# Attention products as four 32-token strips, with the queries turned together with the attention weights

## The chip, the cores and the metric

The kernel runs on one core of a Trainium2 chip, all in float32. The metric is the device time of one execution in microseconds (us); the time before is the median of 12 runs.

## The reference, cut to what matters

Cross-attention and a layer of mixed experts over 4 x 1024 tokens of width 256. The queries come from the normalised tokens, keys and values from a context of 77 rows per batch; 16 heads of 64. Then every token takes two of nine experts (256 to 704 and back).

```python
ln = layernorm(layernorm(x), ln2_w, ln2_b)      # 4 x 1024 x 256: queries
q  = (ln @ Wq) * (1 + scale) + shift            # 16 heads of 64
k, v = split(layernorm(ctx, ln1_w, ln1_b) @ Wkv)
attn = softmax(q @ k.T / 8)                     # 1024 x 77 for each head and batch
x = x + (attn @ v) @ Wout
y = layernorm(x)
x = x + sum over top 2 of 9 experts: w_e * (silu(y @ Wg[e]) * (y @ Wu[e])) @ Wd[e]
```

## The kernel before

**Folded weights.** Before the loop the kernel folds Wq and the keys into one matrix `g` per batch (256 x 1232, plus nine columns for the router), and the values and Wout into `u` (1280 x 265: ten blocks of 128 keys, KC = 10, and 265 = 256 outputs and nine router columns). So for a block of 128 tokens attention is two sets of products: scores = z times `g`, and values = weights times `u`.

**The loop.** There are 32 token blocks (eight groups of four). The instructions stand in the order in which the code calls them; each engine works through its own in that order, and the transfers named here are all issued by SyncE (SP) into one queue. Iteration i does, on TensorE in this order:

- `scores(i, 0)` (L285), six heads of scores, 462 columns;
- `query_turn(i + 1)` (L272), which turns the next block's normalised queries z from tokens by channels into channels by tokens, with two transposing products into `pz`; ScalarE copies them to `zT` (L274), which is the stationary operand of the scores;
- `scores(i, 1)`, `scores(i, 2)` (462 and 317 columns);
- `values(i - 3)` (L361), ten products of 265 columns whose stationary operand is `aT`, the turned attention weights of block i - 3 (LAG = 3).

Iterations 1 to 4 hold left-over preparation too (`extra`): context values and the products for `u` on 64x64 parts of the array. Every fourth iteration has the two small rank products of the router (`ranks`, L1017 and L1020).

Around them: VectorE takes the maxima of the scores (L289); ScalarE the exponentials (L300); VectorE multiplies with the reciprocal sums into the one tile `an` (L322, L327), and `weights_turn(i - 1)` (L341) turns `an` in blocks of 32x32 into `anT`. The turn writes each word ten words from the one before, since the block of keys is the innermost index:

```python
turned = pools["qpool"].tile([P, NQ, Q, KC], F32, tag="anT", name=f"anT{i}", bufs=1)
nc.vector.transpose(
    turned.rearrange("p q t k -> p q k t"), an_of[0].rearrange("p (k q t) -> p q k t", q=NQ, t=Q)
)
nc.sync.dma_start(out=a_d[i % 2], in_=turned.rearrange("p q t k -> p (q t k)"))
```

A turn of 32x32 blocks is not a turn of 128x128, so SyncE stores `anT` to `a_d` in device memory (L344, 640 KB) and `weights_back(i - 1)`, at the end of iteration i, loads it again with the blocks in their places as `aT` (L352, four loads of 160 KB). `aT` has two buffers. Ahead of `weights_back` in SyncE's queue stand, in some iterations, the loads of x (L220), the stores of the sum x (L927) and of the normalised y (L967; these wait for ScalarE), in iteration 1 the 1060 KB of `u_d` (L828), and near the end of the loop the first experts' weights (L1344 to L1354).

`query(i + 2)` (L263) is ScalarE's normalisation of the block after next, into one of two tiles `zs`.

**The experts.** The expert stage (`hidden_pair` L1421, `hidden_thin` L1449, `hidden_one` L1486, `down` L1516) follows the loop and is not changed, apart from the two rank products that fall into it. In `hidden_one` and `down` a block that two or four experts share is worked on in strips of 64 or 32 columns of the array. The strip is chosen by the partitions of the output.

Of the kernel before, what the change touches and what calls it, by code (L numbers as in the profile page):

```python
# [8 lines left out]
F32 = mybir.dt.float32  # L9
I32 = mybir.dt.int32  # L10
U32 = mybir.dt.uint32
AF = mybir.ActivationFunctionType
# [3 lines left out]
P = 128  # L16
# [5 lines left out]
def kernel(  # L22
# [30 lines left out]
    NS = TB // P  # L53
    NG = TOK // TB
    GPB = N // TB
# [3 lines left out]
    JA = 64  # L59
    JR = J - JA  # L60
    NR = 2
    HR = H // NR
    KC = NP + NR
    W = 16
    N2 = NP // 2
    NA = KC * P
    DE = D + E
    HB = TB // J
    banks = [(h, min(HB, H - h)) for h in range(0, H, HB)]
# [46 lines left out]
    ones = const.tile([P, P], F32, name="ones")  # L116
# [76 lines left out]
    pools = {}  # L193


    zs, an_of, lines = [], [], []

    def open_attention():
        for name, bufs in (("qpool", 2), ("rpool", 2)):
            pools[name] = attention.enter_context(tc.tile_pool(name=name, bufs=bufs, side="right"))  # L200
        q = pools["qpool"]
        zs.extend(q.tile([P, D], F32, name=f"z{i}", bufs=1) for i in range(2))
        an_of.append(q.tile([P, NA], F32, name="an", bufs=1))
        for z in zs:
            nc.gpsimd.memset(z[:, D - 1 : D], 1.0)
        for i in range(3):
            lines.append(
                [q.tile([P, NS, WORDS], F32, name=f"line{i}_{k}", bufs=1) for k in range(2)]
            )
            for t in lines[-1]:  # L210
                nc.gpsimd.memset(t.bitcast(I32), NOWHERE)
        for an in an_of:
            nc.gpsimd.memset(an[:, H * JA :], 0.0)

    xg = {}
    pools["xpool"] = attention.enter_context(tc.tile_pool(name="xpool", bufs=4, side="right"))
# [40 lines left out]
    zTs, exs, sms, lgs, aTs, nmx, fstats, pscs = {}, {}, {}, {}, {}, {}, {}, {}  # L257

    def query(i):

        g, s = divmod(i, NS)
        o, r, _ = zscale[g]
        nc.scalar.activation(  # L263
            zs[i % 2][:, : D - 1], xg[g][:, s, : D - 1], AF.Identity,
            bias=o[:, s : s + 1], scale=r[:, s : s + 1],
        )

    def query_turn(i):
# [4 lines left out]
        zT = zTs[i] = pools["qpool"].tile([P, C, P], F32, tag="zT", name=f"zT{i}")  # L273
        nc.scalar.copy(zT.rearrange("p c t -> p (c t)"), pz[:, : C * P])  # L274

    def scores(i, k):

        zT = zTs[i]
        h, n = banks[k]
        if k == 0:  # L280
            nmx[i] = stat.tile([P, H], F32, tag="mx", name=f"mx{i}")
        psc = pscs[k] = ps_sc.tile([P, TB], F32, tag=f"sc{k}", name=f"psc{i}_{k}")
        w = n * J + (E if h + n == H else 0)
        for c in range(C):
            nc.tensor.matmul(  # L285
                psc[:, :w], zT[:, c, :], g_sb[i // NS // GPB][:, c, h * J : h * J + w],
                start=(c == 0), stop=(c == C - 1),
            )
        nc.vector.tensor_reduce(  # L289
            nmx[i][:, h : h + n], psc[:, : n * J].rearrange("p (h j) -> p h j", h=n), AX.X,  # L290
            ALU.max, negate=True,
        )
# [23 lines left out]
    def attention_weights(i):  # L316

        ex, sm = exs.pop(i), sms.pop(i)
        rs = stat.tile([P, H], F32, tag="rs", name=f"rs{i}")
        nc.vector.reciprocal(rs, sm)  # L320
# [6 lines left out]
        nc.vector.tensor_tensor(  # L327
            an[:, H * JA :].rearrange("p (m w n) -> p n m w", w=W, n=N2)[:, :, :, :JR],
            ex[:, :, JA:J].rearrange("p (n m) j -> p n m j", n=N2),
            rs.rearrange("p (n m) -> p n m", n=N2).unsqueeze(3).to_broadcast([P, N2, four, JR]),  # L330
            ALU.mult,
        )

    Q = 32
    NQ = P // Q

    def weights_turn(i):


        turned = pools["qpool"].tile([P, NQ, Q, KC], F32, tag="anT", name=f"anT{i}", bufs=1)  # L340
        nc.vector.transpose(  # L341
            turned.rearrange("p q t k -> p q k t"), an_of[0].rearrange("p (k q t) -> p q k t", q=NQ, t=Q)
        )
        nc.sync.dma_start(out=a_d[i % 2], in_=turned.rearrange("p q t k -> p (q t k)"))  # L344

    def weights_back(i):

        aT = aTs[i] = pools["qpool"].tile([P, NQ, Q * KC], F32, tag="aT", name=f"aT{i}")
        there = a_d[i % 2]
        by_key = there.rearrange("(a i) (q m) -> q i a m", i=Q, q=NQ)  # L350
        for q in range(NQ):
            nc.sync.dma_start(out=aT[q * Q : (q + 1) * Q], in_=by_key[q])  # L352

    pos = {}

    def values(i):
        b = i // NS // GPB
        aT = aTs.pop(i).rearrange("p a (t k) -> p (a t) k", k=KC)
        po = pos[i] = mm_tile(f"po{i}")
        for n in range(KC):  # L360
            nc.tensor.matmul(  # L361
                po[:, :DE], aT[:, :, n], u_sb[b][:, n, :], start=(n == 0), stop=(n == KC - 1)
            )

    def attended(i):
# [15 lines left out]
    with ExitStack() as kvs:  # L381
# [60 lines left out]
        cT = vside.tile([P, C, B * J], F32, name="cT")  # L442
# [121 lines left out]
        for n in range(NP):  # L564
            pk = bank_tile(f"pk{n}")
            for c in range(C):
                nc.tensor.matmul(
                    pk[:, : B * J], wk_sb[:, c, n * P : (n + 1) * P], cT[:, c, :],
                    start=(c == 0), stop=(c == C - 1),
# [5 lines left out]
            while n and pks:  # L575
                m, pk = pks.pop(0)
# [9 lines left out]
            k = n - TURN  # L586
# [50 lines left out]
        def router_weights(pm):  # L637
# [69 lines left out]
        for n in range(NP):  # L707
# [7 lines left out]
            for c in range(C):  # L715
                for t in range(2):
# [4 lines left out]
                        start=True, stop=True,  # L721
                    )
                    h = place_of(n, t)
# [65 lines left out]
        def context_values(k, new=mm_tile):  # L789
            n = k // 2 + k % 2 * N2  # L790
            pv = new(f"pv{n}")
            for c in range(C):
                nc.tensor.matmul(
                    pv[:, : B * J], wv_sb[:, c, n * P : (n + 1) * P], cT[:, c, :],
                    start=(c == 0), stop=(c == C - 1),
                )
# [82 lines left out]
    def rest_of_keys(*ns, last=False):  # L879
# [134 lines left out]
    def ranks(g):  # L1014
        pp = routed[g]["pp"] = mm_tile(f"pp{g}")
        sel, cums = routed[g]["sel"], routed[g]["cums"]
        nc.tensor.matmul(  # L1017
            pp[:, : NS * E], before, sel.rearrange("p s e -> p (s e)"), start=True, stop=False
        )
        nc.tensor.matmul(  # L1020
            pp[:, : NS * E], ones, cums.rearrange("p s e -> p (s e)"), start=False, stop=True
        )

    def places(g):

# [591 lines left out]
        ranks(g)  # L1617
        yield from places(g)

    N_SUB = NG * NS  # L1620
    LAG = 3
    chosen, early = None, None
    for i in range(N_SUB + 1):
        g, s = divmod(i, NS)
# [29 lines left out]
        if now_on:  # L1654
            if i:
                scores(i, 2)
                exponentials(i, 2)
                queries_logits(i)
            if i < N_SUB - 2:
                query(i + 2)  # L1660
            if i:
                extra(i, 2)
            if i == END:
                vsides.close()
        else:
            turn(0)
# [134 lines left out]
```

## Time and profile before

| what | value |
|---|---|
| median of 12 runs | 853.38 us (852.65 to 854.88) |
| the profiled execution: its time, its span | 853.94 us, 852.2 us |
| TensorE granted clock, mean | 0.998 |
| attention loop, scores of iteration 0 to values of block 31 | 36 to 357 us |
| VectorE's turn L341 | 32 of 2.49 us |
| ScalarE's z L263, copy L274 | 32 of 0.61 us, 32 of 0.40 us |
| transfers on SyncE's queue | 158.57 MB, 59.0% of 16 engines' span |

A row of the groups reads: line, engine, operation, output<-inputs, the part of the array (rows*columns, for TensorE), the shape, how many; then busy time and the mean of one in ns; then idle time of the engine in front of them and what ended it. PE is TensorE's products, PEld its weight loads, DVE VectorE, ACT ScalarE, POOL GpSimd, SP SyncE (SPq its DMA queue). A float32 product is two passes in these rows (a transposing product is one). Products are pipelined: the busy mean of one is longer than the step from one start to the next. In a timeline the first number is the start and the second the length, both in us.

### The profile page before, as it was taken

The page shows a single profiled execution, that of the slowest core. Times are in us where ns is not written, and L with a number is a line of the kernel's source. Part 1 is how long each engine was busy: PE and PEld are TensorE (multiplying, and loading weights), DVE is VectorE, ACT ScalarE, POOL GpSimd, SP SyncE. Part 2 cuts the span into 40 slices and gives each one's busy share as a digit, 9 for nine tenths or more (in the row PEclk, how much of TensorE's full clock was granted, in tenths as well). Part 3 has the DMA queues.
Part 4 walks back from the last instruction along what each step waited for, and adds up shares of the span by engine and source line. Part 5 has one row for each costly group of instructions (what it writes and reads, how often), then busy time and mean ns, then how long its engine had stood idle before and what let it go on. Part 6 is the DMA issues. An engine that isn't in the chain of part 4 may idle for free. (4 is left out here: it accounts for less than half of the span.)

```text
span 852.2 us, 14468 instructions
## 1 busy us (share of the span) xinstructions
PE 841.0 (99%) x4148; PEld 674.9 (79%) x4148; DVE 596.4 (70%) x1887; ACT 380.1 (45%) x1570; POOL 311.1 (36%) x344
## 2 busy tenths in 40 slices
PE   8999999999999999999999999999999999999996
PEld 6755877877877878988888879788778878877895
DVE  5777779999989989454854575485578466667550
ACT  4878687978879686252221222222222222222221
POOL 3100000404414140477573454544444453453522
PEclk9999999999999999999999999999999999999999
DMA  8026657566566597896885799789679988788521
GB/s 293 4 108 180 173 180 204 165 218 188 171 195 181 153 264 226 290 306 142 215 240 144 191 339 354 198 238 333 184 225 349 288 224 282 215 246 248 121 25 19
DMA packets 129424, 177.25 MB, mean 208 GB/s; under 512 B 26167, under 2 KB 95295, under 8 KB 129216
## 3 DMA queue, kind: packets, MB, share of 16 engines
q1 hardware_dynamic: 111930, 158.57, 59.0%
q0 software_dynamic: 17344, 17.75, 11.9%
q8 instruction: 33, 0.54, 0.3%
q14 instruction: 47, 0.39, 0.2%
q10 hardware_dynamic: 70, 0.00, 0.0%
HBM read 136.89 MB, written 40.81 MB: 208 GB/s over the span
## 5 line engine op out<-in xcount | busy, mean ns | idle before, releaser
L1421 PE MATMUL pg<-xT,wgu 128*128 128x256 f32 x1100 | 242.7, 379 | 0.1
L1421 PEld LDWEIGHTS pg<-xT,wgu 128*128 128x128 f32 x1100 | 208.5, 190 | 28.7 <-ACT xT L1410 0.7
L1537 POOL DMA_INDIRECT out_dram<-co,ids x73 | 116.0, 1589 | 203.9 <-ACT co L1519 131.1
L300 ACT ACTIVATE ex<-psc,mx 128x77 f32<-128x77 f32 x512 | 159.1, 337 | 64.4 <-DVE mx L289 61.6
L1516 PE MATMUL po<-wd,hid 128*128 128x256 f32 (+2 forms) x768 | 173.2, 380 | 0.0
L1516 PEld LDWEIGHTS po<-wd,hid 128*128 128x128 f32 (+2 forms) x768 | 138.7, 183 | 28.6 <-issue 6.2
L361 PE MATMUL po<-u,aT 128*128 128x265 f32 x640 | 152.2, 393 | 0.8 <-DMA aT<-a_d 0.8
L361 PEld LDWEIGHTS po<-u,aT 128*128 128x128 f32 x640 | 149.6, 311 | 4.1 <-issue 1.7
L1394 DVE STREAM_TRANSPOSE xT<-yin 32x128 f32<-32x128 f32 (+1 forms) x528 | 144.7, 274 | 9.0
L1049 POOL DMA_INDIRECT list_d<-line,r_pli x64 | 66.7, 1042 | 229.8 <-DVE r_pli L1036 120.4
L285 PE MATMUL psc<-g,zT 128*128 128x462 f32 (+1 forms) x384 | 146.7, 513 | 0.0
L1428 DVE TENSOR_TENSOR hid<-pg,sl 128x256 f32<-128x256 f32 x130 | 55.0, 423 | 117.2 <-ACT sl L1427 115.7
L1427 ACT ACTIVATE sl<-pg 128x256 f32<-128x256 f32 x130 | 49.7, 383 | 176.5 <-PE pg L1421 169.5
L300 ACT ACTIVATION_READ_ACCUMULATOR ex<-psc,mx 128x1 f32 x512 | 111.2, 218 | 0.0
L285 PEld LDWEIGHTS psc<-g,zT 128*128 128x128 f32 x384 | 69.7, 190 | 42.9 <-issue 34.3
L1519 ACT ACTIVATE co<-po,ids 128x256 f32<-128x256 f32 x66 | 31.1, 473 | 123.9 <-PE po L1516 121.0
L341 DVE STREAM_TRANSPOSE anT<-an 128x1280 f32<-128x1280 f32 x32 | 79.7, 2492 | 1.9 <-DMA a_d<-anT 1.9
L1361 POOL DMA_INDIRECT yin<-y_d,ids x66 | 69.3, 1051 | 31.6 <-issue 15.6
L289 DVE TENSOR_REDUCE mx<-psc 128x6 f32<-128x462 f32 (+1 forms) x96 | 53.6, 558 | 18.5 <-PE psc L285 18.5
L1506 DVE STREAM_TRANSPOSE hid<-hs 32x160 f32<-32x160 f32 (+1 forms) x112 | 39.5, 353 | 1.7
L322 DVE TENSOR_TENSOR an<-ex,rs 128x1024 f32<-128x1024 f32 x32 | 39.3, 1229 | 1.1
L1449 PEld LDWEIGHTS pt<-xT,wgu 128*128 128x128 f32 x308 | 35.1, 192 | 2.1 <-issue 2.0
(370 smaller groups left out, 766.8 us busy)
## 6 DMA issues: line engine op xcount, KB each, us to landing
wgu<-in_L_ffn_Wg_dram SPq DMA_DIRECT2D x33, 704.0 KB
wd<-in_L_ffn_Wd_dram SPq DMA_DIRECT2D x33, 640.0 KB
a_d<-anT SPq DMA_DIRECT2D x32, 640.0 KB
aT<-a_d SPq DMA_DIRECT2D x128, 160.0 KB
wgu<-in_L_ffn_Wu_dram SPq DMA_DIRECT2D x33, 512.0 KB
w_up<-in_L_ffn_Wg_dram SPq DMA_DIRECT2D x12, 704.0 KB
d_up<-in_L_ffn_Wd_dram SPq DMA_DIRECT2D x12, 640.0 KB
w_up<-in_L_ffn_Wu_dram SPq DMA_DIRECT2D x12, 512.0 KB
```

Of the source, the lines that this page charges most:

```text
L285: nc.tensor.matmul(psc[:, :w], zT[:, c, :], g_sb[i // NS // GPB][:, c, h * J : h * J + w], start=(c == 0), stop=(c == C - 1),)
L289: nc.vector.tensor_reduce(nmx[i][:, h : h + n], psc[:, : n * J].rearrange("p (h j) -> p h j", h=n), AX.X, ALU.max, negate=True,)
L300: nc.scalar.activation(exs[i][:, h + q, :], pscs[k][:, q * J : (q + 1) * J], AF.Exp, bias=nmx[i][:, h + q : h + q + 1], accum_out=sms[i][: ...
L341: nc.vector.transpose(turned.rearrange("p q t k -> p q k t"), an_of[0].rearrange("p (k q t) -> p q k t", q=NQ, t=Q))
L361: nc.tensor.matmul(po[:, :DE], aT[:, :, n], u_sb[b][:, n, :], start=(n == 0), stop=(n == KC - 1))
L1049: i = nc.gpsimd.indirect_dma_start(out=list_d[:, :], out_offset=bass.IndirectOffsetOnAxis(ap=place_i[:, s : s + 1], axis=0), in_=entry.bit ...
L1361: return nc.gpsimd.indirect_dma_start(out=dst, out_offset=None, in_=src, in_offset=bass.IndirectOffsetOnAxis(ap=offsets, axis=0), **kw,)
L1394: yield nc.vector.transpose(xT[q : q + Q].rearrange("p c (h t) -> p h c t", t=P)[:, :nh, :, a : a + Q], of(yins, j)[a : a + Q].rearrange(" ...
L1421: nc.tensor.matmul(pg[:, g, :], w[:, c, at : at + P], xT[:, c, :], start=(c == 0), stop=(c == C - 1),)
L1428: made = nc.vector.tensor_tensor(hid[:, f, :], pg[:, 1, :], sl, ALU.mult)
L1516: nc.tensor.matmul(po[rows, :D], hid[:, f, at], d[:, f, :], start=(f == 0), stop=(f == NF))
L1537: i = nc.gpsimd.indirect_dma_start(out=out_r, out_offset=bass.IndirectOffsetOnAxis(ap=ids[j][:, h, word : word + 1], axis=0), in_=cos[j][: ...
```

## The change

- Scores, values, ranks and most of the context-value products are issued as four products of 32 stationary columns each, one for each strip of 32 tokens (32 rows of the output), all with the same moving operand (`strips`).
- From block 3 on, the normalised queries are not turned by TensorE. ScalarE writes z of block i + 3 into 256 more columns of `an` (KT = KC + C = 12 blocks of 128); VectorE's turn, the store and the loads carry it along, and `scores(i + 3)` read it from `aT` of block i. `query_turn` stays for blocks 0 to 2.
- The turn writes runs of 32 words: the innermost index of `anT` and `aT` is the token in its strip, and no longer the block of keys.

```diff
-    a_d = [dram.tile([P, NA], F32, name=f"a_d{i}") for i in range(2)]
+    a_d = [dram.tile([P, KT * P], F32, name=f"a_d{i}") for i in range(2)]
...
+    def strips(out, left, right, **kw):
+
+        for a in range(0, P, Q):
+            nc.tensor.matmul(out[a : a + Q], left(a), right, **kw)
...
+        z = zs[i % 2] if i < LAG else an_of[0][:, NA:]
...
+    def turned_query(i, c):
+
+        if i < LAG:
+            return lambda a: zTs[i][:, c, a : a + Q]
+        return lambda a: aTs[i - LAG][:, a // Q, KC + c, :]
...
-            nc.tensor.matmul(
-                psc[:, :w], zT[:, c, :], g_sb[i // NS // GPB][:, c, h * J : h * J + w],
+            strips(
+                psc[:, :w], turned_query(i, c), g_sb[i // NS // GPB][:, c, h * J : h * J + w],
...
-        turned = pools["qpool"].tile([P, NQ, Q, KC], F32, tag="anT", name=f"anT{i}", bufs=1)
-        nc.vector.transpose(
-            turned.rearrange("p q t k -> p q k t"), an_of[0].rearrange("p (k q t) -> p q k t", q=NQ, t=Q)
-        )
-        nc.sync.dma_start(out=a_d[i % 2], in_=turned.rearrange("p q t k -> p (q t k)"))
+        turned = pools["qpool"].tile([P, NQ, KT, Q], F32, tag="anT", name=f"anT{i}", bufs=1)
+        nc.vector.transpose(turned, an_of[0].rearrange("p (k q t) -> p q k t", q=NQ, t=Q))
+        nc.sync.dma_start(out=a_d[i % 2], in_=turned.rearrange("p q k t -> p (q k t)"))
...
-        aT = aTs[i] = pools["qpool"].tile([P, NQ, Q * KC], F32, tag="aT", name=f"aT{i}")
+        aT = aTs[i] = pools["qpool"].tile([P, NQ, KT, Q], F32, tag="aT", name=f"aT{i}")
...
         for q in range(NQ):
-            nc.sync.dma_start(out=aT[q * Q : (q + 1) * Q], in_=by_key[q])
+            nc.sync.dma_start(
+                out=aT[q * Q : (q + 1) * Q].rearrange("i a k t -> i a (k t)"), in_=by_key[q]
+            )
...
         for n in range(KC):
-            nc.tensor.matmul(
-                po[:, :DE], aT[:, :, n], u_sb[b][:, n, :], start=(n == 0), stop=(n == KC - 1)
+            strips(
+                po[:, :DE], lambda a: aT[:, a // Q, n, :], u_sb[b][:, n, :],
+                start=(n == 0), stop=(n == KC - 1),
             )
...
-        nc.tensor.matmul(
-            pp[:, : NS * E], before, sel.rearrange("p s e -> p (s e)"), start=True, stop=False
-        )
-        nc.tensor.matmul(
-            pp[:, : NS * E], ones, cums.rearrange("p s e -> p (s e)"), start=False, stop=True
-        )
+        for k, (w, what) in enumerate(((before, sel), (ones, cums))):
+            strips(
+                pp[:, : NS * E], lambda a: w[:, a : a + Q], what.rearrange("p s e -> p (s e)"),
+                start=(k == 0), stop=(k == 1),
+            )
...
-            if 0 < i < N_SUB - 1:
+            if 0 < i < LAG - 1:
                 query_turn(i + 1)
...
-            if i < N_SUB - 2:
-                query(i + 2)
+            for j in (2, LAG) if not i else (i + LAG,) if i + LAG < N_SUB else ():
+                query(j)
```

`context_values` makes the same replacement for all but its first two products, and GpSimd presets one more column of ones.

More of the change, by code (lines that the diff above doesn't have):

```diff
@@ L66 @@
     NA = KC * P
+    KT = KC + C
+    Q = 32
+    NQ = P // Q
+    N_SUB = NG * NS
+    LAG = 3
     DE = D + E
@@ L202, in open_attention @@
         zs.extend(q.tile([P, D], F32, name=f"z{i}", bufs=1) for i in range(2))
-        an_of.append(q.tile([P, NA], F32, name="an", bufs=1))
-        for z in zs:
+        an_of.append(q.tile([P, KT * P], F32, name="an", bufs=1))
+        for z in zs + [an_of[0][:, NA:]]:
             nc.gpsimd.memset(z[:, D - 1 : D], 1.0)
@@ L212, in open_attention @@
         for an in an_of:
-            nc.gpsimd.memset(an[:, H * JA :], 0.0)
+            nc.gpsimd.memset(an[:, H * JA : NA], 0.0)
     xg = {}
@@ L262, in query @@
         o, r, _ = zscale[g]
+        z = zs[i % 2] if i < LAG else an_of[0][:, NA:]
         nc.scalar.activation(
-            zs[i % 2][:, : D - 1], xg[g][:, s, : D - 1], AF.Identity,
+            z[:, : D - 1], xg[g][:, s, : D - 1], AF.Identity,
             bias=o[:, s : s + 1], scale=r[:, s : s + 1],
@@ L274, in query_turn @@
         nc.scalar.copy(zT.rearrange("p c t -> p (c t)"), pz[:, : C * P])
+    def turned_query(i, c):
+        if i < LAG:
+            return lambda a: zTs[i][:, c, a : a + Q]
+        return lambda a: aTs[i - LAG][:, a // Q, KC + c, :]
     def scores(i, k):
-        zT = zTs[i]
         h, n = banks[k]
@@ L327, in attention_weights @@
         nc.vector.tensor_tensor(
-            an[:, H * JA :].rearrange("p (m w n) -> p n m w", w=W, n=N2)[:, :, :, :JR],
+            an[:, H * JA : NA].rearrange("p (m w n) -> p n m w", w=W, n=N2)[:, :, :, :JR],
             ex[:, :, JA:J].rearrange("p (n m) j -> p n m j", n=N2),
@@ L332, in attention_weights @@
         )
-    Q = 32
-    NQ = P // Q
     def weights_turn(i):
-        turned = pools["qpool"].tile([P, NQ, Q, KC], F32, tag="anT", name=f"anT{i}", bufs=1)
-        nc.vector.transpose(
-            turned.rearrange("p q t k -> p q k t"), an_of[0].rearrange("p (k q t) -> p q k t", q=NQ, t=Q)
-        )
-        nc.sync.dma_start(out=a_d[i % 2], in_=turned.rearrange("p q t k -> p (q t k)"))
+        turned = pools["qpool"].tile([P, NQ, KT, Q], F32, tag="anT", name=f"anT{i}", bufs=1)
+        nc.vector.transpose(turned, an_of[0].rearrange("p (k q t) -> p q k t", q=NQ, t=Q))
+        nc.sync.dma_start(out=a_d[i % 2], in_=turned.rearrange("p q k t -> p (q k t)"))
     def weights_back(i):
-        aT = aTs[i] = pools["qpool"].tile([P, NQ, Q * KC], F32, tag="aT", name=f"aT{i}")
+        aT = aTs[i] = pools["qpool"].tile([P, NQ, KT, Q], F32, tag="aT", name=f"aT{i}")
         there = a_d[i % 2]
@@ L357, in values @@
         b = i // NS // GPB
-        aT = aTs.pop(i).rearrange("p a (t k) -> p (a t) k", k=KC)
+        aT = aTs.pop(i)
         po = pos[i] = mm_tile(f"po{i}")
         for n in range(KC):
-            nc.tensor.matmul(
-                po[:, :DE], aT[:, :, n], u_sb[b][:, n, :], start=(n == 0), stop=(n == KC - 1)
+            strips(
+                po[:, :DE], lambda a: aT[:, a // Q, n, :], u_sb[b][:, n, :],
+                start=(n == 0), stop=(n == KC - 1),
             )
@@ L792, in context_values @@
             for c in range(C):
-                nc.tensor.matmul(
-                    pv[:, : B * J], wv_sb[:, c, n * P : (n + 1) * P], cT[:, c, :],
-                    start=(c == 0), stop=(c == C - 1),
-                )
+                w, kw = wv_sb[:, c, n * P : (n + 1) * P], dict(start=(c == 0), stop=(c == C - 1))
+                if k < 2:
+                    nc.tensor.matmul(pv[:, : B * J], w, cT[:, c, :], **kw)
+                else:
+                    strips(pv[:, : B * J], lambda a: w[:, a : a + Q], cT[:, c, :], **kw)
             src = pv[:, : B * J].rearrange("p (b j) -> p b j", b=B)
@@ L1016, in ranks @@
         sel, cums = routed[g]["sel"], routed[g]["cums"]
-        nc.tensor.matmul(
-            pp[:, : NS * E], before, sel.rearrange("p s e -> p (s e)"), start=True, stop=False
-        )
-        nc.tensor.matmul(
-            pp[:, : NS * E], ones, cums.rearrange("p s e -> p (s e)"), start=False, stop=True
-        )
+        for k, (w, what) in enumerate(((before, sel), (ones, cums))):
[3 more added lines that the diff above has]
+            )
     def places(g):
@@ L1618, in listed @@
         yield from places(g)
-    N_SUB = NG * NS
-    LAG = 3
     chosen, early = None, None
```

## The prediction

> **What bounds the kernel now.** I read the page's engine table first, then the groups with shapes kept apart, then the timeline of TensorE and of SyncE's queue.
>
> ```profile
> PE 841.0 (99%) x4148; PEld 674.9 (79%) x4148; DVE 596.4 (70%) x1887; ACT 380.1 (45%) x1570; POOL 311.1 (36%) x344
> ```
>
> TensorE (PE) has work from end to end, so a saved product shortens the run, and so does nothing else; a wait put into its queue lengthens it one for one. The busy mean of a product (379 ns for 256 columns) holds its pipelined tail. Its price is the step from one start to the next, which the timeline gives (start, length, engine, line, count):
>
> ```profile
> 202.79 4.74 PE L361 MATMUL po<-u,aT 128*128 128x265 f32 x20
> 207.36 1.71 PE L285 MATMUL psc<-g,zT 128*128 128x462 f32 x4
> 208.91 0.38 PE L272 MATMUL pz<-ident,z 128*128 128x128 f32 x2
> 209.13 2.78 PE L285 MATMUL psc<-g,zT 128*128 128x462 f32 x8
> ```
>
> Values: 4.57 us for 20 passes (a product is two passes), 228 ns each. Scores: 1.55 us for four, 388 ns each at 462 columns (267 at 317, single instructions). The two turns of a query: 0.22 us, 109 ns each. One iteration is 8.95 us, and from 100 to 300 us TensorE waits for nothing. 462 columns in 388, 308 in 259, 256 in 216 ns lie on one line, columns/1.2 plus 2.5 to 3 ns; on it 265 columns would take 223.5, so the values pay 4.5 ns extra. The groups say why:
>
> ```profile
> L361 PEld LDWEIGHTS po<-u,aT 128*128 128x128 f32 x640 | 149.6, 311 | 4.1 <-issue 1.7 <-ACT u L151 0.4
> L285 PEld LDWEIGHTS psc<-g,zT 128*128 128x128 f32 x384 | 69.7, 190 | 42.9 <-issue 34.3 <-DVE rs L320 1.4 <-DVE mx L289 0.4
> ```
>
> Same size, but the load whose elements lie ten words apart takes 311 ns, 121 more.
>
> **Strips.** The kernel already has four 32-column strips, in the down products of the shared blocks:
>
> ```profile
> 568.01 0.38 PE L1421 MATMUL pg<-xT,wgu 128*128 128x256 f32 x1
> 568.32 0.40 PE L1516 MATMUL po<-wd,hid 128*32 128x256 f32 x1
> 568.32 0.42 PE L1516 MATMUL po<-d_up,hid 128*32 128x256 f32 x3
> 568.56 0.38 PE L1516 MATMUL po<-wd,hid 128*32 128x256 f32 x1
> 568.56 0.39 PE L1516 MATMUL po<-d_up,hid 128*32 128x256 f32 x3
> 568.77 0.38 PE L1516 MATMUL po<-wd,hid 128*32 128x256 f32 x1
> ```
>
> The four start within 20 ns and the next four 0.21 to 0.24 us later (217 ns in the run of them), against 216 for one whole pass. So a group of four costs what one pass costs: between -2.5 ns (if the fixed part vanished) and +1 ns on 1,024 groups, -2.6 to +1.0 us; I take 0. These rows have four different moving operands, the change has one read four times; that is not shown. PE's passes grow from 4148 to some 7340 and its instruction packets (33 on the page) to under 60; no wait for them shows at 27 ns per instruction in the rows above, but those runs are short.
>
> [...] The rows at 568 us decide for 217 ns.
>
> Now the sum, on the profiled execution's own 853.94 us (span 852.2).
>
> - Values: strips are loaded from 32 adjacent elements, so 228 becomes 223.5 on 640 groups: **-2.9**.
> - Query turns 3 to 31 leave TensorE: 58 x 109 ns: **-6.3**. ScalarE loses 29 copies of 0.40 us; it is not the bound and that is worth nothing by itself.
> - Rank products: 32 passes of 108 to 112 ns (36 columns, bound by loading). As strips between 33 ns (36/1.2 + 3) and 112: 0 to -2.5; I take **-1.0**.
> - Changes of tile shape: at 568.01 to 568.32 the step is 0.31 instead of 0.216, 0.09 more. The program has 50 changes of column shape on TensorE and gets 66: **+1.3** (16 x 0.093, less 0.1 for each of two fewer returns to the whole array).
>
> Together -8.9; an iteration shrinks by 0.31 to 8.64 us.
>
> - VectorE's turn grows from 1280 to 1536 elements but writes runs of 32 words instead of steps of ten:
>
> ```profile
> L341 DVE STREAM_TRANSPOSE anT<-an 128x1280 f32<-128x1280 f32 x32 | 79.7, 2492 | 1.9 <-DMA a_d<-anT 1.9
> L1394 DVE STREAM_TRANSPOSE xT<-yin 32x128 f32<-32x128 f32 x304 | 92.0, 303 | 5.0
> L1394 DVE STREAM_TRANSPOSE xT<-yin 32x64 f32<-32x64 f32 x224 | 52.7, 235 | 4.0
> ```
>
> L1394 writes such runs: 64 more elements cost 68 ns, 1.06 ns each, so 167 + 1536 x 1.06 = 1.80 us. At today's 1.95 ns each it would be 2.99. I take 1.80, 0.69 less, as the layout of the writes is that of L1394. VectorE is busy 223 of the 250 us from 80 to 330 and stays below TensorE.
>
> - Off the path: z of block i+3 is made by ScalarE where z of i+2 was (32 of 0.61 us, as now), into a strip of `an` that VectorE's turn in the same iteration has left by then: its next reader comes some 4 us into the next iteration. One more memset on GpSimd, and the context values as strips: nothing. SyncE issues the same 160 transfers.
>
> - **The new wait.** Values of token block d ask for aT at the end of iteration d+3; scores of block d+3 now ask for the same tile at its beginning, 4.4 us earlier, and everything on TensorE queues behind them. The way there: turn, store to a_d, four loads of aT, all in SyncE's one queue behind other transfers:
>
> ```profile
> 196.77 0.34 SPq L344 DMA_DIRECT2D a_d<-anT  x1
> 201.28 0.34 SPq L967 DMA_DIRECT2D y_d<-y  x1
> 201.72 2.98 SPq L352 DMA_DIRECT2D aT<-a_d  x4
> ```
>
> This is block 15: its last packet ends at 208.21 (from the trace's DMA packets of 1280 bytes), values began at 211.75, but scores of iteration 18 began at 207.36. And after landing TensorE needs 0.88 us more: block 27's last packet ends at 321.25, and the one such wait of today ends at 322.14:
>
> ```profile
> 322.14 1.03 PE L361 MATMUL po<-u,aT 128*128 128x265 f32 x3 [0.78 <-DMA aT<-a_d]
> ```
>
> End of aT's read less start of scores three iterations on, before: iteration 3 +3.6 us; 7 -0.6; 10 -0.8; 14 +0.9; 18 +0.85; 22 -0.5; 26 -0.1; 29 +3.6; 30 +4.4; 31 +0.8; the rest -1.7 or lower. (Every fourth iteration the y_d store waits for ScalarE and holds up aT; iteration 3 stands behind the 1060 KB of u_d; 29 and 30 behind expert weights.) To each add: 0.88 to start; 0.63 for two shorter iterations; -0.69 for the turn; the read of 768 instead of 640 KB, undisturbed 3.1 us, 0 to +0.64, I take 0.45; the store (about 2 us), +0.33 where aT waits for it and not for y_d. That is +1.27, or +1.60 with the store. Waits: iteration 3: 4.9; 7: 1.0; 10: 0.5; 14: 2.2; 18: 2.1; 22: 0.8; 26: 1.1; 29: 5.2; 30: 1.8 (5.7 less the 5.2 already lost, and 1.3 because its store stands in the queue behind the late read); 31: 0.3. In all 19.9, less 0.9 and 0.2 of waits at 322 and 312 us that go: **+18.8**. Bounds: without the read's growth and with half the 0.88, about +11; with a turn of 2.99 us all of these grow by 1.19 and seven more appear, about +34.
>
> Sum: 853.94 - 8.9 + 18.8 = 863.8; the runs' median is 0.56 below the profiled execution, so **863.3**.
>
> The waits of 5 us could cost twice. In the rows by windows TensorE's granted clock is still 1.00 from 846 to 848 us and 0.85 from 848 to 849, its last product having ended at 844.1: it fell after 4.6 us of idleness. If it falls in iterations 3 and 29, about 4 us at half speed (the length of the first products at 427 ns steps) lose 2 us each, +4; I leave this to the range. [...]
>
> **Rivals.**
> 1. *aT is early enough* (faster). One mechanism: everything from the end of VectorE's turn to the first product runs earlier against the scores than I reckon. It decides when the waits add up to less than 8.9 us, that is when the read ends some 1.5 us sooner than in my list. For it: the faster turn, and ScalarE's 0.40 us, which y_d waits for. Against it: iterations 3 and 29 alone were late by 3.6 us each before anything is added. Price: down to 853.4 - 8.9 = 844.5.
> 2. *The turn stays at 1.95 ns an element, or the clock falls as well.* Waits of 25 to 34: 870 to 879.
> 3. *Strips with one moving operand do not run alongside, or their instructions come too slowly.* One tenth more on 276 us of strips is +28: 890 and beyond.
> 4. *Gain and waits cancel*, 852 to 855.
>
> **How the numbers follow.** Forecast (857 to 870) 0.61, rival 1 0.13, rival 4 0.07, rival 2 0.14, rival 3 0.05. A difference of 0.2%, 1.7 us, is about what measuring this kernel can tell. Faster 0.13, same 0.07, slower 0.80. The range reaches from the cancelling case to most of rival 2: 851 to 878; it leaves out nearly all of rivals 1 and 3 and a tail.
>
> **What would show it.** Right: two pz groups less per iteration and groups of four 7 ns apart with 223 to 224 ns between groups of the values; a turn of 128x1536 in 1.8 us; TensorE idle before scores with "DMA aT<-a_d" as releaser, 4 to 5 us in iterations 3 and 29, 1 to 2 us every fourth iteration. Wrong: no such idle time (rival 1), a turn near 3 us or a granted clock of 0.5 there (rival 2), groups above 230 ns (rival 3).

## The result, and the profile after

The changed kernel took 865.69 us (median of 7 runs, 862.61 to 868.07) against 853.20 for the kernel before (28 runs): ratio 1.0144, 95% interval 1.0132 to 1.0155, 12.5 us slower. A second measurement, beside three of the experiments, gave 864.29 (861.63 to 871.24) against 853.33, ratio 1.0143 (1.0111 to 1.0175). The profiled execution took 863.34 us with a span of 861.6, 9.4 more than before; it is one of the shorter runs, 2.35 below the median.

The experiments ran in three sets of runs, each with the kernel before beside it (the second measurement is part of the second set); in the first and the third that kernel itself took 871.0 and 872.0 us, so times are compared inside a set only.

The engine row of the page after:

```profile
PE 835.8 (97%) x7330; PEld 598.9 (70%) x7330; DVE 579.2 (67%) x1887; ACT 374.9 (44%) x1541; POOL 311.4 (36%) x345
```

TensorE has 5 us less to do and a span 9.4 us longer: 99% busy has become 97%. The groups with shapes kept apart (busy, mean ns of one, idle before and its releaser) say where the gap is, and what strips and turn cost:

```profile
L141 PE MATMUL po<-u,aT 128*32 128x265 f32 x2560 | 150.0, 386 | 0.2 <-DMA aT<-a_d 0.2
L141 PE MATMUL psc<-g,aT 128*32 128x462 f32 x928 | 99.3, 566 | 15.6 <-DMA aT<-a_d 13.3 <-DVE r_top L1003 1.2 <-DVE r_o L1000 1.0
L354 DVE STREAM_TRANSPOSE anT<-an 128x1536 f32<-128x1536 f32 x32 | 56.6, 1768 | 0.0
```

The idle time sits before the scores (15.6 us) and no longer before the values, and what ends it is the load of `aT`. Where `r_top` and `r_o` are named, VectorE had long been done: the starts are 0.7 to 0.9 us behind the last packet of `aT` there too (0.5 to 1.0 over all the waits). The turn of 1536 elements takes 1.77 us. The longest wait, in TensorE's timeline:

```profile
63.83 0.67 PE L823 MATMUL pu<-wo_sb,vals 64*64 64x265 f32 x6 [0.15 <-ACT u L161]
69.45 3.09 PE L141 MATMUL psc<-g,aT 128*32 128x462 f32 x16 [4.96 <-DMA aT<-a_d]
72.48 1.13 PE L823 MATMUL pu<-wo_sb,vals 64*64 64x265 f32 x16
```

That is iteration 3. The first scores behind the wait take 3.1 us instead of 1.6, because the clock had fallen. In the windows (stretch, length, busy time and count of each engine, granted clock, DMA share, GB/s) it stands at 0.50 there, and a second time behind the wait of iteration 29:

```profile
70.00:72.00 2.00, 2.00 (x16) 0.39 (x8) 0.00 (x0) 0.00 (x0) 0.00 (x0) 0.50 0.41 126
318.00:320.00 2.00, 2.00 (x16) 0.80 (x12) 0.86 (x3) 0.22 (x2) 0.00 (x0) 0.50 0.98 278
```

From the starts of the single products, the terms of the span are:

| term | forecast, us | measured, us | from |
|---|---|---|---|
| values, 640 groups | -2.9 | -3.2 | 228 to 223 ns a group |
| query turns | -6.3 | -6.3 | 58 products gone, 109 ns each |
| rank products | -1.0 | -1.5 | six places in the loop, 0.25 us each |
| 16 more changes of shape | +1.3 | (+1.3) | carried over, not measured |
| waits of the scores | +19.9 | +17.5 | excess over the usual step, summed |
| waits of before that go | -1.1 | -1.1 | |
| half clock | 0 (in the range) | +2.7 | longer steps at 0.5, 1.4 and 1.3 us |
| sum | +9.9 | +9.4 | span 852.2 to 861.6 |

The usual step here is that of the kernel before, 0.23 us; against the 0.17 to 0.20 of strips the waits come to 18.1. So the sum closes to some half a us, with one term carried over. That it lies so near the forecast is in part luck: the waits came 2.4 us short, and the half clock, forecast at nothing, brought 2.7.

### The profile page after: what moved, and what is told of

Its sections match the earlier page's. It is cut to its first block, busy times and chain, and to the rows that moved or that the text cites. A ratio compares the mean times of both kernels' runs of the same rounds, so it can differ in the third digit from the quotient of the medians.

```text
span 861.6 us, 20822 instructions
## 1 busy us (share of the span) xinstructions
PE 835.8 (97%) x7330; PEld 598.9 (70%) x7330; DVE 579.2 (67%) x1887; ACT 374.9 (44%) x1541; POOL 311.4 (36%) x345
## 5 line engine op out<-in xcount | busy, mean ns | idle before, releaser
L141 PE MATMUL po<-u,aT 128*32 128x265 f32 x2560 | 150.0, 386 | 0.2 <-DMA aT<-a_d 0.2
L141 PE MATMUL psc<-g,aT 128*32 128x462 f32 (+1 forms) x1392 | 131.5, 521 | 15.6 <-DMA aT<-a_d 13.3
L141 PEld LDWEIGHTS po<-u,aT 128*32 128x32 f32 x2560 | 96.1, 110 | 49.7 <-issue 0.8
L141 PEld LDWEIGHTS psc<-g,aT 128*32 128x32 f32 x1392 | 50.8, 111 | 84.1 <-issue 57.7
L316 ACT ACTIVATION_READ_ACCUMULATOR ex<-psc,mx 128x1 f32 x512 | 106.4, 208 | 0.0
L354 DVE STREAM_TRANSPOSE anT<-an 128x1536 f32<-128x1536 f32 x32 | 56.6, 1768 | 0.0
```

The source lines that it names most:

```text
L141: nc.tensor.matmul(out[a : a + Q], left(a), right, **kw)
L316: nc.scalar.activation(exs[i][:, h + q, :], pscs[k][:, q * J : (q + 1) * J], AF.Exp, bias=nmx[i][:, h + q : h + q + 1], accum_out=sms[i][: ...
L354: nc.vector.transpose(turned, an_of[0].rearrange("p (k q t) -> p q k t", q=NQ, t=Q))
```

## The experiments

### Is it the wait? Scores one block later

Scores(i) read the queries from `aT` of block i - 4 instead of i - 3, so the tile is an iteration older when it is needed. `aT` gets a third buffer, which is paid for by letting other tiles share or lose a buffer, and the scale of the queries is called earlier in the iteration.

```diff
+    QLAG = 4
...
-        return lambda a: aTs[i - LAG][:, a // Q, KC + c, :]
+        return lambda a: aTs[i - QLAG][:, a // Q, KC + c, :]
...
-        aT = aTs[i] = pools["qpool"].tile([P, NQ, KT, Q], F32, tag="aT", name=f"aT{i}")
+        aT = aTs[i] = pools["qpool"].tile([P, NQ, KT, Q], F32, tag="aT", name=f"aT{i}", bufs=3)
...
-            for j in (2, LAG) if not i else (i + LAG,) if i + LAG < N_SUB else ():
+            for j in (2, QLAG) if not i else (3, 5) if i == 1 else (i + QLAG,) if i + QLAG < N_SUB else ():
```

> As the change, but ScalarE makes z of block i+4 in iteration i (not i+3), so scores read the queries from the aT of four blocks before, one iteration (8.6 us) after they land; aT has three buffers (paid for by laying z and zT of the first four blocks into the tile of y and by single buffers for five small router tiles). TensorE turns blocks 0 to 3. Theory A: no waits in front of scores but perhaps 1 to 2 us in front of values near iterations 29 and 30: 853.2 - 8.7 + 0 to 3 = 844 to 848 us, clock 1.00 throughout the loop. Theory B (strips cost, or the larger transfers slow the loop): at or above 853.

Measured in the first set: 900.72 us against 870.99, ratio 1.0349 (1.0312 to 1.0387); this spoke for neither theory until the trace was read (below, instructions). In the second set:

> Scores one block later, so that they wait for aT(i-4). Theory (the wait of the scores costs 17.6 us and 2.7 us of half clock, the rest of the change gains 8.9): 20 us below the changed kernel on the same chip, 844 to 848 where before takes 853 (ratio to before 0.99 to 0.995). Rival (the strips themselves cost the time): no faster than the changed kernel, 863 to 868. Where the strips starve, both lie some 25 us higher, and the gap between the two stays 15 to 20.

Measured: 847.76 us against 853.33, ratio 0.9934 (0.9921 to 0.9947), and 16.5 us below the changed kernel in the same set. TensorE's list of waits for `aT` (total, times, longest) in the changed kernel of that set and in this one:

```profile
PE psc L141 <- DMA aT<-a_d: 12.3, 6, 5.1
```

```profile
PE po L142 <- DMA aT<-a_d: 3.9, 4, 1.4
```

The scores wait for nothing; the values wait for blocks 26, 27, 29 and 30, where the experts' weights load. The clock does not fall before the loop and the experts are done (mean granted clock 0.997, against 0.991 in the changed kernel beside it). 852.2 - 9.7 (the first four terms above) - 1.1 + 4.4 (the wait of the values as longer steps) gives 845.8; the span is 845.4. The changed kernel beside it has a span of 862.7. So the loss is the wait, and the rest of the change is a gain.

### The wait alone

The kernel before, with one unread product of 8 columns ahead of scores(i):

```diff
         if now_on:
+            if d >= 0:
+                nc.tensor.matmul(
+                    mm_tile(f"hold{i}")[:, :8], aTs[d][:, 0, :P], g_sb[i // NS // GPB][:, 0, :8],
+                    start=True, stop=True,
+                )
             if i:
                 scores(i, 0)
```

> The kernel before with one addition: ahead of scores(i), from iteration 3 on, one unread product of 8 columns that reads aT(i-3). It puts the wait of the changed kernel in front of the scores, and nothing else: no strips, no turned queries, values stay at the end of the iteration. The 29 added products cost 0.1 to 0.3 us each, 3 to 9 us. Theory (the wait for aT(i-3) at the head of the iteration is what costs): from before's own margins (end of aT's read less start of scores three iterations on, plus 0.9 us) waits of 4.5 us in iterations 3 and 29, 1.7 in 14 and 18, below 1 in 7, 10, 22, 26, some 15 us with iterations 30 and 31, and about 3 us of half clock: 868 to 878 where before takes 853. Rival (the longer turn and transfer of the queries are what costs): 856 to 862, the added products alone.

Measured (third set): 891.57 us against 871.97, ratio 1.0232 (1.0209 to 1.0256), 19.6 us. The wait in iteration 3:

```profile
68.80 0.57 PE L1633 MATMUL hold<-g,aT 128*128 128x8 f32 x2 [3.88 <-DMA aT<-a_d]
```

Within the loop an iteration takes 9.17 us instead of 8.95, so the 29 added products cost some 6.1; the waits in front of them, from the starts, are 4.0, 0.5, 0.4, 0.7, 2.6 and 2.3 us in iterations 3, 14, 18, 26, 29 and 30, together 10.4, and the products at half clock behind two of them (granted clock 0.50 from 69 to 73 us) 3.1. Less the 1.0 of before's own waits that go, that is 18.6. The loop, from scores(0) to the values of block 31, takes 340.7 us against 321.4 in before's trace, 19.3 longer. (The experts, which are the same in both, take 513.0 us here and 494.8 in before's trace, about the 18.6 us by which the kernel before itself is longer in this set.) So the wait alone, without strips and turned queries, loses as much as the theory said. The waits are smaller than in the changed kernel (10.4 for 17.5), perhaps because the added products stretch each iteration; that was not tested.

### Values first: a longer loop than I had seen

```diff
+        if now_on and d >= 0:
+            values(d)
...
-        if d >= 0:
+        if d >= 0 and not now_on:
             values(d)
```

The two added lines stand at the head of the iteration, ahead of scores(i).

> The kernel before, with one thing moved: in each iteration values(i-3) go in front of scores(i) instead of behind them, so that the first TensorE product of the iteration needs aT(i-3). No strips, no turned queries. Theory (the change loses its time by having the first product of an iteration wait for aT(i-3)): the waits of before grow by the 2.8 us of scores that no longer cover them, some 15 us in all, 866 to 870 where before takes 853 (ratio 1.015 to 1.02). Rival (what costs is the longer turn and transfer of the queries, not the order): 853 to 857.

Measured: 919.59 us against 853.33, ratio 1.0775 (1.0761 to 1.0789): four times what I expected, and not explained by before's margins. The waits (total, times, longest) and one iteration of VectorE:

```profile
PE po L361 <- DMA aT<-a_d: 44.5, 19, 5.6
```

```profile
223.20 0.64 DVE L289 TENSOR_REDUCE mx<-psc 128x6 f32<-128x462 f32 x1 [1.43 <-PE psc L285]
...
226.07 2.49 DVE L341 STREAM_TRANSPOSE anT<-an 128x1280 f32<-128x1280 f32 x1
```

VectorE's turn of block i - 1 stands behind the maxima of the scores of block i. So what delays scores(i) delays aT(i-1), which TensorE needs two iterations later: a loop. Here: values(14) start at 225.84, scores(17) behind them at 230.41, the turn of block 16 runs from 235.03 to 237.46, its `aT` has landed at 245.16, and 0.8 us later values(16) could start. That is 20.1 us for two iterations whose work is 17.9, even where nothing else is in SyncE's queue. This reading of the trace was not tested by a run of its own; what the run shows is that moving before's margins by hand did not give the time.

In the changed kernel the same loop starts at the scores. In the second set scores(14) start at 177.60, the turn of block 13 runs from 182.30 to 184.07, its `aT` has landed at 192.90, and 0.7 us later scores(16) could start: 16.0 us against 17.3 of work. It has 1.3 us to spare, and any transfer that holds `aT` up by more than that becomes a wait.

### Strips alone

The kernel before with the strips of 32 columns in the same places as the changed kernel, and nothing else: queries turned by TensorE, the words of a token side by side.

```diff
-            nc.tensor.matmul(
-                po[:, :DE], aT[:, :, n], u_sb[b][:, n, :], start=(n == 0), stop=(n == KC - 1)
+            strips(
+                po[:, :DE], lambda a: aT[:, a : a + 32, n], u_sb[b][:, n, :], start=(n == 0), stop=(n == KC - 1)
             )
```

(and so for scores, ranks and context values)

> The kernel before, with its attention products, the rank products and the later products of the table split into four strips of 32 columns and nothing else: queries still turned by TensorE, weights still turned word by word with ten words between the tokens of a strip. Theory (a group of four strips costs what one pass costs): 850 to 854 where before takes 853: -1.0 for the ranks, 0 to -2.9 for the values (it is open whether the stride of 40 bytes still costs 4.5 ns a group), +1.3 to +4 for changes of shape, of which the TensorE turns between strips add two each iteration. [...] Where TensorE starves for instructions in GpSimd's bursts: some 25 us above before.

Measured: 857.76 us against 853.33, ratio 1.0051 (1.0038 to 1.0064), 4.4 us slower, above the 850 to 854 given. The timeline around the turns of the queries:

```profile
154.32 1.73 PE L136 MATMUL psc<-g,zT 128*32 128x462 f32 x16
155.99 0.44 PE L277 MATMUL pz<-ident,z 128*128 128x128 f32 x2
156.35 2.83 PE L136 MATMUL psc<-g,zT 128*32 128x462 f32 x32
```

From strips to the turns it is 1.67 us and back 0.36, against 1.55 and 0.22 in the kernel before: 0.12 and 0.14 for two changes of shape, 0.26 in each iteration. In some 30 iterations that is 7.8 us, where the expectation had at most 4; with -3.2 and -1.5 for values and ranks and 1.1 for longer waits of the values it makes +4.2 (the spans differ by 5.0). The values step by 223 ns here as well, although a strip's elements still lie ten words apart (the mean load of a strip is 137 ns in this kernel's groups, 110 in the changed kernel's).

### Turned queries alone

Queries turned with the weights, but whole passes of 128 columns, and the words of a token side by side as before, now twelve of them:

```diff
-        turned = pools["qpool"].tile([P, NQ, Q, KC], F32, tag="anT", name=f"anT{i}", bufs=1)
+        turned = pools["qpool"].tile([P, NQ, Q, KT], F32, tag="anT", name=f"anT{i}", bufs=1)
```

> The queries are turned with the weights, but products stay whole (128 columns) and the word-by-word layout of before stays, so VectorE's turn writes steps of twelve words. Theory A: turns of TensorE -6.3 us; values stay at 228 ns; VectorE's turn 1536 x 1.95 ns = 2.99 us, 1.2 us later than in the change, so the waits of the scores grow by about 1.2 us wherever they were and appear in more iterations: 870 to 882 us. Theory B (strips are what costs): faster than the change, near 860 or below.

Measured in the first set: 905.56 us against 870.99, ratio 1.0378 (1.0354 to 1.0401). Once more in the third set:

> Turned queries without strips: whole passes of 128 columns, the old layout with the words of a token side by side, turn and transfer of 1536 elements. Theory: the values keep 228 ns a pass, the queries' turns leave TensorE (-6.3), the turn takes 1536 x 1.95 = 2.99 us instead of 1.77, so the waits are those of the changed kernel and 1.2 us more in every iteration that waits, with seven more iterations waiting: 870 to 882 where before takes 853. On the chip where the kernel before took 871 it was 34.6 us above before. Rival (the turn's length doesn't matter, the order alone does): as the changed kernel, 863 to 868.

Measured: 907.13 us against 871.97, ratio 1.0391 (1.0369 to 1.0414), 35 us instead of 17 to 29. Groups and timeline of the third set:

```profile
L364 PEld LDWEIGHTS po<-u,aT 128*128 128x128 f32 x640 | 174.0, 368 | 0.5 <-ACT u L154 0.4
L344 DVE STREAM_TRANSPOSE anT<-an 128x1536 f32<-128x1536 f32 x32 | 93.1, 2911 | 0.0
```

```profile
201.20 5.48 PE L364 MATMUL po<-u,aT 128*128 128x265 f32 x20
206.51 4.37 PE L288 MATMUL psc<-g,aT 128*128 128x462 f32 x12
```

The turn took 2.91 us, as the theory said. But the values did not keep 228 ns: 20 passes take 5.31 us, 266 each, beside loads that take 368 ns at twelve words' distance where they took 311 at ten. That is 0.76 us in an iteration, some 24 us, which the expectation had missed. With iterations of 9.53 us the waits of the scores come to 10 us, less than in the changed kernel. All of the 35 us lie in the loop: it takes 356.4 us against 321.4 in before's trace. So the queries cannot be carried along in the old layout for nothing; in the new one, with strips, they can. Whole passes that read the new layout, as four runs of 32 words, were not run, so it is not shown that the strips are needed for it.

### Strips and the new layout, queries still turned by TensorE

```diff
-    KT = KC + C
+    KT = KC
...
-        z = zs[i % 2] if i < LAG else an_of[0][:, NA:]
+        z = zs[i % 2]
```

> Strips and runs of 32 as in the change, but the queries are turned by TensorE into zT as before (the store and the loads carry 640 KB again). Theory A (the loss is the scores' wait for aT): those waits are gone; values 640 x -4.5 ns = -2.9 us, ranks -1, but the two turns of each iteration now stand as whole-array products between strips, two more changes of shape in each of 29 iterations at 0.093 us plus 0.1 us for the return to the whole array: +8. About 857 us, no idle time in front of scores. Theory B (strips themselves cost): the steps between groups are longer than 223 and 387 ns, well above 860 us.

Measured in the first set: 914.00 us against 870.99, ratio 1.0503 (1.0474 to 1.0531). As a time it decides nothing between the theories, since its strips waited for instructions (see next). But the trace ahead of the first such stop, up to 160 us, agrees with theory A: scores(3), (8) and (10), which wait 5.0, 0.9 and 1.3 us in the changed kernel, start without a wait, and an iteration takes 9.15 us, as with strips alone (9.16).

### Instructions that come too slowly

The values of the kernel with the scores one block later, in the first set (900.72 us) and in the second (847.76):

```profile
L142 PE MATMUL po<-u,aT 128*32 128x265 f32 x2560 | 177.8, 394 | 17.8 <-issue 16.0
```

```profile
L142 PE MATMUL po<-u,aT 128*32 128x265 f32 x2560 | 149.9, 387 | 3.9 <-DMA aT<-a_d 3.9
```

The same kernel, and 16 us of idle time that nothing but "issue" ends: TensorE waits there for nothing that the profile shows. TensorE's and GpSimd's timeline of the first:

```profile
160.76 0.61 PE L142 MATMUL po<-u,aT 128*32 128x265 f32 x2 [0.84 <-issue]
```

```profile
151.80 1.12 POOL L1065 DMA_INDIRECT list_d<-line,r_pli  x1 [116.67 <-DVE r_pli L1052]
...
161.42 0.98 POOL L1065 DMA_INDIRECT list_d<-line,r_pli  x1 [0.31 <-issue]
```

TensorE stands still where GpSimd issues its indirect stores in a row. In this kernel that begins some 150 to 165 instructions (products and loads) after the first store of a row, in four rows between 152 and 291 us; with the queries turned by TensorE it begins after 165, 103, 101 and 97. Between 152 and 167 us the trace has no packet in the instruction queue whose packets grow with the strips (queue 8 of the page, from 33 to 58); in the second set one comes at 161.7, and the same rows of stores do no harm. That the instructions come too slowly is read from this; no run tested it. Strips use up instructions four times as fast as whole passes: the kernel with the wait alone, all in whole passes in its loop, came through these rows in the third set, and stood still only in the experts, some 177 instructions into a long row. Why it happens in two sets and not in the third, the runs do not show. The changed kernel itself was not run in those sets; the two kernels nearest to it, which follow, had ratios of 1.048 to 1.050 there.

### Waits filled, for the clock

The changed kernel with unread strip products ahead of scores(3) and scores(29):

```diff
+            for _ in range({LAG: 11, 29: 6}.get(i, 0)):
+                strips(
+                    mm_tile(f"hold{i}_{_}")[:, :462], lambda a: ones[:, a : a + Q], g_sb[i // NS // GPB][:, 0, :462],
+                    start=True, stop=True,
+                )
```

> As the change, with products that nobody reads (strips of 462 columns, 0.39 us a group) in front of the scores of iteration 3 (eleven groups, 4.3 us) and 29 (six, 2.3 us), where TensorE waits in any case. Theory A, with the clock's fall as a part of it: waits end when they did, the clock stays at 1.00 and two stretches of 3.4 us at half speed are gone: 1.7 to 3.4 us less than the change, about 862.5. If the clock's fall costs nothing, the same time as the change or up to 1 us more where the filling outlasts a wait.

Measured in the first set: 915.67 us against 870.99, ratio 1.0495 (1.0474 to 1.0517). Again in the third:

> The changed kernel with unread strip products ahead of scores(3) and scores(29), which keep TensorE busy through the two longest waits (11 groups of 0.39 us and 6 of them). The read of aT is not touched. Theory (the clock falls because TensorE stands idle there, and each fall costs 1.3 to 1.4 us): no stretch at clock 0.5, 2 to 3 us less than the changed kernel, 861 to 864 where before takes 853. Rival (the clock falls for another reason, or the fall costs nothing): clock 0.5 in the same places or no gain, 864 to 868. If the added products run past the end of the wait they cost what they run over.

Measured: 914.57 us against 871.97, ratio 1.0480 (1.0454 to 1.0505). The times are those of strips that wait for instructions and decide nothing, but iteration 3 lies ahead of all rows of stores:

```profile
64.55 8.73 PE L141 MATMUL hold<-g,ones 128*32 128x462 f32 x88
73.10 1.73 PE L141 MATMUL psc<-g,aT 128*32 128x462 f32 x16
...
81.64 1.55 PE L141 MATMUL po<-u,aT 128*32 128x265 f32 x24
```

I had priced a product as one pass; the eleven groups are 22 and took 8.5 us, 3.5 longer than the wait. But the clock stays at 1.00 throughout iteration 3, and from its first scores to the values it is 8.54 us instead of 9.91 and 10.07 in the two profiles of the changed kernel. In the next experiment's kernel, of the same set and not filled, the clock falls at 66.47 us, in that wait. So standing still is what lowers the clock there, and the fall in iteration 3 costs 1.4 to 1.5 us. Iteration 29 lies behind the first of the rows of stores and can't be compared.

### The store of y_d in another queue

```diff
-        nc.sync.dma_start(out=y_d.rearrange("(g p s) d -> g p s d", p=P, s=NS)[g], in_=y)
+        nc.scalar.dma_start(out=y_d.rearrange("(g p s) d -> g p s d", p=P, s=NS)[g], in_=y)
```

> The changed kernel with the store of y_d issued by ScalarE's queue, behind the operation that makes y, instead of by SyncE's. In SyncE's queue it waits for ScalarE in every fourth iteration, and the four loads of aT wait behind it. Theory (that is what makes the scores wait in iterations 10, 14, 18, 22 and 26): these five waits of 1 to 1.6 us shrink to under 0.5, 4 to 6 us less than the changed kernel: 859 to 862 where before takes 853 (ratio 1.007 to 1.010). Rival (they wait because the store and read are slow beside other transfers): 863 to 866 as before. The waits in iterations 3 and 29 stay in either case.

Measured (third set): 914.17 us against 871.97, ratio 1.0479 (1.0460 to 1.0497); as a time it says nothing for the same reason. Block 7 lies ahead of the rows of stores. SyncE's queue in the changed kernel (second set) and here:

```profile
129.23 0.34 SPq L355 DMA_DIRECT2D a_d<-anT  x1
133.85 0.34 SPq L982 DMA_DIRECT2D y_d<-y  x1
134.28 2.21 SPq L363 DMA_DIRECT2D aT<-a_d  x4
```

```profile
128.65 0.34 SPq L355 DMA_DIRECT2D a_d<-anT  x1
132.97 2.45 SPq L363 DMA_DIRECT2D aT<-a_d  x4
```

The loads are issued 4.3 us behind the store of `anT` instead of 5.1, but take 7.1 us to land instead of 6.5, and scores(10) wait 1.27 us instead of 1.36. In this one block the queue was not the limit: y_d's packets meet `aT`'s either way. The other blocks can't be compared, and the theory stays open for them.

## Why the prediction was right, and where its steps were not

The forecast of 863.3 us is 2.4 below the median, and the mechanism is the one it named: a gain near 9 us, and a new wait of the scores for `aT`, about twice as large. For the profiled execution it reckoned 863.8, which took 863.34; what makes the median run longer than that one, no trace shows.

- **Strips cost nothing in a stream:** 223 ns a group at 265 columns, as the down products (217 at 256) had shown. Their shape changes were sized from one row (0.09 us); beside whole-array products they measure 0.12 to 0.14.
- **Values, right number, wrong reason.** The step "strips are loaded from 32 adjacent elements, so 228 becomes 223.5" gave the cause to the layout. With strips on the old layout the group takes 223 ns too: splitting the load was enough.
- **The turn** was bounded by 1.80 and 2.99 us and took 1.77. The upper end is that of the old layout: 2.91 with turned queries alone.
- **The waits:** the total was close (17.5 for 19.9), the list was not. Iteration 3 had 5.0 for 4.9, iteration 7 none for 1.0, iterations 10, 14, 18, 22 and 26 had 1.3, 1.6, 1.0, 1.0 and 1.2 for 0.5, 2.2, 2.1, 0.8 and 1.1; but 29, 30 and 31 had 2.5, 0 and 0 for 5.2, 1.8 and 0.3, and 8, 21, 23, 25 and 28, which were not on the list, had 3.9 together. In the second profile iteration 7 waits 1.0, 22 waits 2.6, and 21 and 28 do not wait, so the list differs from one execution to the next too. The step that failed took each margin of before by itself. A late read of one block holds up the next store in the same queue; I had priced this for iteration 30 only:

```profile
110.03 0.34 SPq L355 DMA_DIRECT2D a_d<-anT  x1
115.41 1.73 SPq L363 DMA_DIRECT2D aT<-a_d  x4
```

Block 4's read ends at 111.53, after block 5's store was issued at 110.03; block 5's loads follow 5.4 us behind its store, instead of 3.3 undisturbed, and scores(8) wait 0.9 us. With 1.3 us to spare in the loop, that is enough. (The 0.3 us for iteration 31 has no working beside it, and none came.)

- **The clock** was the one term left to the range, and the reading behind it was wrong. "It fell after 4.6 us of idleness" was taken from one place at the end; in iteration 29 the clock fell to 0.50 behind a wait of 2.5 us. The cost of 2.7 us lies inside the "+4" that was left to the range. A clock of 0.5 there was to be a sign of rival 2; the sign came, without the 870 us and more of that rival.
- **Rival 3's second half,** instructions that come too slowly, was named and given 0.05 together with its first. It did not occur where the changed kernel was measured, and it did in two sets of experiments, at 30 us and more.

## What to carry to other kernels

Before you let the first product of an iteration read what the last one read before, follow the whole loop back to that product (here scores, maxima, the turn queued behind them, store, load, 0.7 us to start) and set it against the iterations it has; the slack of that loop, and not the single margins of the old schedule, says what each disturbance in the queue will cost. One more buffer and one block of lag turned +11 us into -5.6 us (ratio 0.9934), the fastest version here, though only where the instructions kept up. Splitting products into more instructions was free on the array here, and in two of three sets it was not free: TensorE stood still for want, as it reads, of instructions.

## What the runs showed of the hardware that was not expected

- **The clock changed in steps of 3.413 us.** In the first trace of the changed kernel the stretches from one change of TensorE's granted clock to the next are 61.44 us at 1.00, 3.41 at 0.50, 245.76 at 1.00, 3.41 at 0.50 and 535.89 at 1.00: 18, 1, 72, 1 and 157 times 3.413. The one such stretch of the kernel before is 843.09 us, 247 times. In the changed kernel's second profile the clock fell at 65.89 us, only 1.3 us after TensorE's last product, and stayed down for 6.83 us; in its first at 68.78, 4.3 us after it, for 3.41. A wait of 2.6 us in iteration 22 of the second profile did not lower it at all. So what a wait cost in clock did not follow from its length; that its place against these steps decides it was not shown. The runs of the changed kernel scatter over 5.5 us (9.6 in the second measurement) where those of the kernel before scatter over 2.4; that the clock is the cause was not shown either.
- **Distance between the elements of a load** (128 columns, mean of the group): 190 ns for adjacent words (scores of the kernel before), 311 for ten words apart (its values), 368 for twelve (values with turned queries alone). The pass of 265 columns above it takes 223.5 (reckoned from the steps at 256, 308 and 462 columns), 228 and 266 ns.
- **VectorE's turn** took 1.15 ns an element where it writes runs of 32 words (the changed kernel, 1768 ns for 1536) and 1.90 where it writes single words twelve apart (turned queries alone, 2911).
- **TensorE can stand still** some 100 to 180 instructions into a row of GpSimd's indirect stores, with nothing to wait for that the profile shows, in some sets of runs and not in others.
